# A four-layer graph network kernel: one halved group instead of two, loads in the order of need, new planned times, and a later way back in the recurrence

## The chip, the cores and the metric

The kernel runs on one core of one Trainium2 chip. The metric is the device time of one launch in microseconds (us), the median over runs. PE is TensorE, DVE is VectorE, ACT is ScalarE, POOL is GpSimd. "L306" is line 306 of the kernel whose profile is read; because the change moves lines, the same code has other numbers further down the file (the third layer's wide product is L618 in the kernel before and L627 in the changed one).

## The reference

128 graphs of 64 nodes with 256 features pass through four layers, each with a layernorm and relu ahead and a residual addition behind:

```python
for layer in (gat4, gat1, relational, gated):        # (shortened)
    h = relu(layernorm(x))
    x = x + layer(h, adj)

# gat4: softmax over neighbours, 4 heads of 64; gat1: one head of 256
# relational: only relation 1 occurs in a 0/1 adjacency:
#   relu(adj.T @ ((h W.T + b) * sigmoid(h W.T Wg.T + bg)))
# gated: three steps of
#   aggr = adj.T @ (h @ weight[i]);  h = GRU(aggr, h)
```

The three GRU steps are most of TensorE's work. They form a chain: each step needs the state of the step before.

## The kernel before

The 64 tiles of 128 rows (two graphs each) are worked on in 16 groups of 4 tiles. For each group there is a job per layer (`first_layer`, `second_layer`, `third_layer`), a job `before` (layernorm, transposes and first aggregation for the GRU), and a job `recur` (the three GRU steps). A job is a generator that emits instructions and yields its estimated TensorE time. `Weave` runs the jobs against a virtual clock: each job has a planned start and end, and the job that is most behind emits next. While the recurrence of group g is emitted, the layer jobs of group g+3 or so fill the places in between. The result is one fixed order for each engine, in which the engine then works.

```python
plan = Weave()
plan.add("weights", 14.0, 86.0, 24.0, 0.0, later_weights(early))
...
start = 103.0
for g in range(NG):
    if g < 2:                                   # groups 0 and 1 are halved
        t = 32.0 * g
        units = [(0, 2, [t + x for x in (0, 32, 60, 84)], 0),
                 (2, 2, [t + x for x in (5, 37, 65, 89)], 3 - g)]   # second half: spare tiles
    elif g < AHEAD:                             # AHEAD = 3
        units = [(0, G, [66.0, 110.0, 150.0, 185.0], 0)]
    else:
        at = 110.0 + 96.0 * (g - AHEAD)         # planned start of a group's layers
        units = [(0, G, [at + 73.0 * i for i in range(4)], 0)]
    ...
for g in range(NG):
    at = start + g * 93.0                       # planned start of a recurrence
    ...
    if g == 0:
        after += ["weights"] + spares           # its tiles lie where the spare ones lay
```

So the layers of group 3 are planned 7 us after the first recurrence's start (110 - 103), with a period of 96 us, against 93 us for the recurrences. I call this offset the phase of the plan. It drifts by 3 us a group, as far as the dependences let it.

One step of the recurrence, for chunk 0 of the new state (features 0 to 127) and then chunk 1:

```python
yield r.add(whh, hT, 0)                 # gates, 128x512 products of 0.86 us each
yield h.add(whh, hT, 0)
yield z.add(whh, hT, 0)
yield r.add(w, aT, 0)
...
yield h.add(whh, hT, 0) + h.add(whh, hT, 1)
hnat = work.tile([P, G, D], F32, name="hnat")
yield back(hnew, hnat, 0, src if last else None)    # way back: transposes (L306), copy (L308)
n = Gate("nn", 5, 2)
yield n.add(w, aT, 0) + n.add(w, aT, 1)
...
if not last:
    new = work.tile([P, K, T], F32, name="aT")
    yield along(psum, hnat, abd, new, 0)            # next aggregation (L264), copy (L268)
yield z.add(w, aT, 0) + z.add(w, aT, 1)
next(second)                                        # last half of the update of chunk 1
```

The attention vectors were loaded one after another into one tile `ab` and multiplied on GpSimd:

```python
def attention_columns(w, heads, pieces, engine):
    for i, a in enumerate(pieces):
        ab = once.tile([P, D], F32, name="ab")
        nc.scalar.dma_start(ab, over_partitions(a, D))
        wa = once.tile([P, K, D], F32, name="wa")
        engine.tensor_tensor(wa, w[:, :, :D], ab[:, None, :].to_broadcast([P, K, D]), ALU.mult)
        ...
```

## Time and profile before

| | before |
|---|---|
| median of 3 runs | 1722.49 us (1721.14 to 1729.14) |
| span of the profiled run, mean granted clock | 1725.0 us, 0.976 |
| TensorE busy | 1596.9 us (93%) |
| TensorE idle before the first recurrence matmul (161.6 us) | 53.1 us |
| TensorE idle from there to its end | 66.7 us |

Idle time of TensorE is the bracketed time ahead of each row of its timeline, summed; the bracket also names what ended it. The view of TensorE's waits collects these brackets over the run. Its columns: engine, tile and line that waited, what it waited for, us in total, times, the longest.

```profile
PE tp L166 <- DVE hn L158: 35.7, 8, 23.2
PE tp L306 <- DVE hT L330: 28.1, 15, 4.8
PE mm L250 <- DVE eb L569: 13.9, 8, 5.6
...
PE rz L295 <- DVE aT L268: 2.9, 3, 2.5
```

The first line is mostly the start: one wait of 23.2 us for the first layernorm. The second is the way back of the recurrence, waiting for the new state from DVE; with 4.9 us in which L306 waited for other things, these are the 33.0 us of the prediction. The third is the attention's aggregation, waiting for exps masked by DVE.

### The profile page before, as it was taken

To read this page: it belongs to the slowest core of one execution; us is meant where nothing else is said; L and a number is where in the kernel's file an instruction comes from. 1 tells how busy PE (TensorE), PEld (TensorE's weight loads), DVE (VectorE), ACT (ScalarE), POOL (GpSimd) and SP (SyncE) were. 2 spreads that over 40 slices of the span, in tenths; PEclk is the share of its full clock that TensorE was granted. 3 is DMA by queue.
4 is the path that set the end of the run, shared out by engine and by line. 5 is a ranking of instruction groups with operands and counts; after the bars stand their busy time and mean duration, and the time that the engine had idled before them with its cause. 6 is when DMAs were issued, how large, how long until landed. Compare 5 with 4: busy or idle time off the path is not lost.

```text
span 1725.0 us, 16160 instructions
## 1 busy us (share of the span) xinstructions
PE 1596.9 (93%) x5689; PEld 902.1 (52%) x5689; DVE 1028.4 (60%) x2401; ACT 472.8 (27%) x910; POOL 279.9 (16%) x254
## 2 busy tenths in 40 slices
PE   4877999999998998989999999999999999999997
PEld 3554555555554554545545555554555545554543
DVE  5766673856667474664647657464665657554433
ACT  2322322222322222223222332322222222222221
POOL 2110110211111011211112212021111111111110
PEclk9977999999999999999999999999999999999998
DMA  7000000000100000000000001000000000000000
GB/s 201 7 3 1 16 4 28 19 28 16 28 19 4 28 19 25 19 28 4 19 25 20 28 3 43 4 16 25 16 13 3 25 0 16 13 4 13 0 13 15
DMA packets 45510, 34.96 MB, mean 20 GB/s; under 512 B 21612, under 2 KB 43756, under 8 KB 45420
## 3 DMA queue, kind: packets, MB, share of 16 engines
q1 hardware_dynamic: 42444, 32.52, 6.7%
q10 hardware_dynamic: 2976, 1.32, 0.3%
q8 instruction: 47, 0.77, 0.2%
q14 instruction: 43, 0.35, 0.1%
HBM read 25.30 MB, written 8.52 MB: 20 GB/s over the span
## 4 chain that ended last, share of the span: by engine, by line
PE 66%; DVE 21%; POOL 5%; issue 3%; ACT 2%; DMA 2%; SPq 0%; POOLq 0%; DVEq 0%; ACTq 0%
PE rz L295 27%; PE nn L295 13%; PE mm L231 6%; PE mm L618 5%; PE mm L250 5%; PE tp L264 4%; DVE hn L158 3%; PE tp L166 3%; DVE st L149 2%; POOL rstd L154 2%; PE tp L306 2%; POOL xg L210 2%; DVE d L329 2%; DVE hT L330 1%; PE mm L630 1%
## 5 line engine op out<-in xcount | busy, mean ns | idle before, releaser
L295 PE MATMUL rz<-hT,whh 128*128 128x512 f32 x768 | 390.8, 600 | 3.9 <-ACT z L328 3.4
L295 PE MATMUL rz<-aT,wc 128*128 128x512 f32 x768 | 388.8, 597 | 3.1 <-DVE aT L268 2.9
L325 POOL TENSOR_TENSOR d<-hT,nt 128x512 f32<-128x512 f32 x96 | 125.1, 1303 | 784.1 <-ACT nt L323 784.1
L295 PEld LDWEIGHTS rz<-aT,wc 128*128 128x128 f32 x768 | 140.2, 191 | 145.4 <-issue 128.3
L295 PEld LDWEIGHTS rz<-hT,whh 128*128 128x128 f32 x768 | 138.5, 192 | 118.9 <-issue 105.5
L295 PE MATMUL nn<-aT,wc 128*128 128x512 f32 x384 | 191.1, 597 | 0.0
L295 PE MATMUL nn<-hT,whh 128*128 128x512 f32 x384 | 190.8, 598 | 0.0
L329 DVE SCALAR_TENSOR_TENSOR d<-z,d 128x512 f32<-128x512 f32 x96 | 74.2, 773 | 102.5 <-POOL d L325 59.1
L158 DVE TENSOR_SCALAR hn<-xg,mv,rstd 128x256 f32<-128x256 f32 x256 | 101.3, 441 | 46.6 <-POOL rstd L154 46.4
L264 PEld LDWEIGHTS tp<-abd,hnat 128*128 128x128 f32 x768 | 102.0, 194 | 43.3 <-issue 31.5
L618 PE MATMUL mm<-wl,hT 128*128 128x512 f32 x248 | 122.1, 617 | 0.3 <-ACT hT L167 0.3
L166 PE MATMUL tp<-ident,hn 128*128 128x128 f32 x512 | 75.5, 285 | 50.3 <-DVE hn L158 35.7
L167 ACT ACTIVATE hT<-tp 128x512 f32<-128x512 f32 (+1 forms) x130 | 69.4, 572 | 190.0 <-PE tp L166 189.8
L149 DVE BATCH_NORM_STATS2 st<-xg 128x6 f32<-128x256 f32 x256 | 98.3, 408 | 30.5 <-POOL xg L210 25.8
L250 PEld LDWEIGHTS mm<-wh,eb 128*128 128x128 f32 x600 | 87.5, 203 | 53.7 <-issue 27.8
L250 PE MATMUL mm<-wh,eb 128*128 128x65 f32 (+1 forms) x600 | 101.8, 305 | 14.5 <-DVE eb L569 13.9
L323 ACT ACTIVATE nt<-t,bi 128x512 f32<-128x512 f32 x96 | 69.2, 720 | 166.7 <-DVE t L321 141.6
L154 POOL TENSOR_TENSOR rstd<-var,mhalf 128x4 f32<-128x4 f32 (+1 forms) x70 | 68.3, 976 | 284.2 <-DVE var L153 277.8
L320 DVE SCALAR_TENSOR_TENSOR t<-r,t 128x512 f32<-128x512 f32 x96 | 67.7, 705 | 73.5 <-ACT r L317 58.7
L264 PE MATMUL tp<-abd,hnat 128*128 128x128 f32 x768 | 103.9, 278 | 3.9 <-DVE hnat L308 2.4
L317 ACT ACTIVATE r<-rz,brz 128x512 f32<-128x512 f32 x96 | 65.8, 686 | 150.4 <-PE rz L295 150.3
L166 PEld LDWEIGHTS tp<-ident,hn 128*128 128x128 f32 x512 | 61.8, 146 | 83.7 <-issue 33.1
(161 smaller groups left out, 1842.6 us busy)
## 6 DMA issues: line engine op xcount, KB each, us to landing
out_dram<-hnat SPq DMA_DIRECT2D x16, 512.0 KB
xg<-in_x_dram SPq DMA_DIRECT2D x15, 512.0 KB
hT<-row SPq DMA_DIRECT2D x26, 256.0 KB
at<-in_adj_dram SPq DMA_DIRECT2D x64, 32.0 KB
ag<-in_adj_dram SPq DMA_DIRECT2D x16, 128.0 KB
t<-row SPq DMA_DIRECT2D x26, 64.0 KB
ihn<-in_L_gnn_w_ih_dram SPq DMA_DIRECT2D x1, 768.0 KB
hhn<-in_L_gnn_w_hh_dram SPq DMA_DIRECT2D x1, 768.0 KB
```

What stands on the lines that cost most here:

```text
L149: nc.vector.bn_stats(st[:, p, :], src[:, p, :])
L154: nc.gpsimd.tensor_tensor(rstd, var, mhalf[:, :n], ALU.pow)
L158: nc.vector.tensor_scalar(hn[:, p, :], src[:, p, :], mv[:, p, 0:1], rstd[:, p : p + 1], op0=ALU.subtract, op1=ALU.mult,)
L166: nc.tensor.transpose(pt[:, p * P : (p + 1) * P], hn[:, p, k * P : (k + 1) * P], ident)
L167: nc.scalar.activation(hT[:, k, :], pt[:, : n * P], AF.Relu)
L231: nc.tensor.matmul(pm[:, : D + 2 * heads], hT[:, k, p * P : (p + 1) * P], we[:, k, :], start=(k == 0), stop=(k == K - 1),)
L250: nc.tensor.matmul(pv[:, h, :], lhsT(p, h), wv[:, p, h, :], start=True, stop=True)
L264: nc.tensor.matmul(pa[:, p * P : (p + 1) * P], hnat[:, p, c * P : (c + 1) * P], abd[:, p, :], start=True, stop=True,)
L295: nc.tensor.matmul(self.pg, w[:, k, self.chunk * P : (self.chunk + 1) * P], m[:, k, :], start=(self.done == 0), stop=(self.done == self.n ...
L325: nc.gpsimd.tensor_tensor(d, hT[:, c, :], nt, ALU.subtract)
L329: nc.vector.scalar_tensor_tensor(d, z, 1.0, d, op0=ALU.add, op1=ALU.mult)
L618: nc.tensor.matmul(pm, hT[:, k, p * P : (p + 1) * P], wl[:, k, :], start=(k == 0), stop=(k == K - 1))
```

## The change

Its intent, in its own words: only the first group is halved, so the recurrence's tiles come free in time; loads come in the order of need; the recurrence's way back of chunk 0 is later. Behind these words are five edits. (a) Group 1 is no longer halved. (b) The plan has new numbers. (c) Group 2 gets its rows by DMA (AHEAD 2). (d) The loads are reordered, with the four attention vectors in slices of one tile and their products on DVE. (e) In the recurrence `back` of chunk 0 moves behind two products, and `along` of chunk 0 moves into the next step.

```diff
+            if i > 0:
+                aT = work.tile([P, K, T], F32, name="aT")
+                yield along(psum, hnat, abd, aT, 0)
             yield r.add(w, aT, 0)
 ...
+            n = Gate("nn", 5, 2)
+            yield n.add(w, aT, 0) + n.add(w, aT, 1)
             hnat = work.tile([P, G, D], F32, name="hnat")
             yield back(hnew, hnat, 0, src if last else None)
-            n = Gate("nn", 5, 2)
-            yield n.add(w, aT, 0) + n.add(w, aT, 1)
 ...
-            if not last:
-                new = work.tile([P, K, T], F32, name="aT")
-                yield along(psum, hnat, abd, new, 0)
             yield z.add(w, aT, 0) + z.add(w, aT, 1)
 ...
-        AHEAD = 3
+        AHEAD = 2
 ...
+        AB = once.tile([P, 4, D], F32, name="AB")
+        for i, a in enumerate((a_src, a_dst)):
+            nc.scalar.dma_start(AB[:, i, :], over_partitions(a, D))
 ...
         load_group(0)
         load_group(1)
+        nc.sync.dma_start(w1e[:, :, :D], rows(W1))
 ...
-        load_group(2)
 ...
-        plan.add("weights", 14.0, 86.0, 24.0, 0.0, later_weights(early))
+        plan.add("clear", 2.5, 3.0, 0.1, 0.0, clear())
+        plan.add("columns", 2.0, 17.0, 0.2, 15.0, first_weights())
+        plan.add("weights", 18.0, 80.0, 24.0, 0.0, later_weights(early))
 ...
-        start = 103.0
+        start, period = 93.0, 93.0
 ...
+            if g == 0:
+                units = [(0, 2, (0.0, 30.0, 56.0, 76.0), False), (2, 2, (4.0, 34.0, 60.0, 80.0), True)]
+            elif g == 1:
+                units = [(0, G, (30.0, 76.0, 116.0, 146.0), False)]
+            elif g == 2:
+                units = [(0, G, (76.0, 130.0, 190.0, 235.0), False)]
             else:
-                at = 110.0 + 96.0 * (g - AHEAD)
-                units = [(0, G, [at + 73.0 * i for i in range(4)], 0)]
+                at = 130.0 + 93.5 * (g - 3)
+                units = [(0, G, [at + 68.0 * i for i in range(4)], False)]
```

More of the change, by code (lines that the diff above doesn't have):

```diff
@@ L377, in recurrence @@
             hT = hnew
-            if not last:
-                aT = new
         yield back(hT, hnat, 1, src)
@@ L448 @@
         load_group(1)
+        nc.sync.dma_start(w1e[:, :, :D], rows(W1))
+        for i, a in enumerate((a1[:D], a1[D:])):
+            nc.sync.dma_start(AB[:, 2 + i, :], over_partitions(a, D))
         wn, gn = loaded(early, "wn", W_loop), loaded(early, "gn", Wg_loop)
         ihn, hhn = loaded(early, "ihn", w_ih), loaded(early, "hhn", w_hh)
-        load_group(2)
-        wrn = [loaded(early, name, weight[i]) for i, name in enumerate(("wrn0", "wrn1", "gn"))]
+        for i, b in enumerate((b_loop, bg_loop)):
+            nc.sync.dma_start(bl[:, i * D : (i + 1) * D], over_partitions(b[0:1], D))
+        with nc.allow_non_contiguous_dma(reason="biases onto partitions"):
+            nc.sync.dma_start(bi, b_ih.rearrange("(c p) -> p c", p=P))
+            nc.sync.dma_start(bh, b_hh.rearrange("(c p) -> p c", p=P))
+        wrn = [loaded(early, name, weight[i]) for i, name in enumerate(("wrn0", "wn", "gn"))]
         make_identity(nc, ident)
@@ L459, with attention_columns @@
         nc.vector.memset(mhalf, -0.5)
-        def attention_columns(w, heads, pieces, engine):
-            for i, a in enumerate(pieces):
-                ab = once.tile([P, D], F32, name="ab")
-                nc.scalar.dma_start(ab, over_partitions(a, D))
+        def attention_columns(w, heads, pieces):
+            for i, ab in enumerate(pieces):
                 wa = once.tile([P, K, D], F32, name="wa")
-                engine.tensor_tensor(wa, w[:, :, :D], ab[:, None, :].to_broadcast([P, K, D]), ALU.mult)
+                nc.vector.tensor_tensor(wa, w[:, :, :D], ab[:, None, :].to_broadcast([P, K, D]), ALU.mult)
                 nc.vector.tensor_reduce(
@@ L471, in attention_columns @@
                 )
-        attention_columns(w0e, H, (a_src, a_dst), nc.gpsimd)
-        nc.scalar.dma_start(w1e[:, :, :D], rows(W1))
-        for i, b in enumerate((b_loop, bg_loop)):
-            nc.scalar.dma_start(bl[:, i * D : (i + 1) * D], over_partitions(b[0:1], D))
-        with nc.allow_non_contiguous_dma(reason="biases onto partitions"):
-            nc.scalar.dma_start(bi, b_ih.rearrange("(c p) -> p c", p=P))
-            nc.scalar.dma_start(bh, b_hh.rearrange("(c p) -> p c", p=P))
+        unset = []
         def blocks(name, n, pool=once):
             t = pool.tile([P, n, P], F32, name=name)
-            nc.gpsimd.memset(t, 0.0)
+            unset.append(t)
             return t
         EB = [blocks("eb0", G * H), blocks("eb1", G)]
-        OH = [blocks(f"oh{i}", G) for i in range(2)]
-        ABD = [blocks(f"abd{i}", G) for i in range(2)]
         wl = once.tile([P, K, 2 * D], F32, name="wl")
@@ L578, in attention, with clear, first_weights @@
             yield -6.0
+        def clear():
+            for t in unset:
+                nc.gpsimd.memset(t, 0.0)
+            yield 0.1
+        def first_weights():
+            attention_columns(w0e, H, (AB[:, 0, :], AB[:, 1, :]))
+            yield 0.1
+            yield -15.0
+            attention_columns(w1e, 1, (AB[:, 2, :], AB[:, 3, :]))
+            yield 0.1
         def later_weights(prep):
-            attention_columns(w1e, 1, (a1[:D], a1[D:]), nc.vector)
-            yield 0.1
             yield from relational_weights(prep, psum, wl, wn, gn, 0.5)
@@ L638 @@
         EBE = [blocks("eb0e", 2 * H, early), blocks("eb1e", 2, early)]
+        OH = [blocks(f"oh{i}", G) for i in range(2)]
+        ABD = [blocks(f"abd{i}", G) for i in range(2)]
         def first_layer(g, p0, n, spare):
@@ L670 @@
         plan = Weave()
-        plan.add("weights", 14.0, 86.0, 24.0, 0.0, later_weights(early))
+        plan.add("clear", 2.5, 3.0, 0.1, 0.0, clear())
+        plan.add("columns", 2.0, 17.0, 0.2, 15.0, first_weights())
+        plan.add("weights", 18.0, 80.0, 24.0, 0.0, later_weights(early))
         layers = (first_layer, second_layer, third_layer)
         work_of, wait_of = (9.0, 8.2, 10.4), (38.0, 35.0, 13.5)
-        users, spares = {}, []
-        start = 103.0
+        start, period = 93.0, 93.0
+        users = {}
         for g in range(NG):
-            if g < 2:
-                t = 32.0 * g
-                units = [(0, 2, [t + x for x in (0, 32, 60, 84)], 0), (2, 2, [t + x for x in (5, 37, 65, 89)], 3 - g)]
-            elif g < AHEAD:
-                units = [(0, G, [66.0, 110.0, 150.0, 185.0], 0)]
-            else:
-                at = 110.0 + 96.0 * (g - AHEAD)
-                units = [(0, G, [at + 73.0 * i for i in range(4)], 0)]
+            if g == 0:
[4 more added lines that the diff above has]
+                units = [(0, G, (76.0, 130.0, 190.0, 235.0), False)]
+            else:
+                at = 130.0 + 93.5 * (g - 3)
+                units = [(0, G, [at + 68.0 * i for i in range(4)], False)]
             for p0, n, at, spare in units:
@@ L688 @@
                     after = [(g, p0, i - 1)] if i > 0 else []
-                    if (i, i < spare) in users:
-                        after.append(users[i, i < spare])
-                    users[i, i < spare] = (g, p0, i)
-                    if i < spare:
-                        spares.append((g, p0, i))
-                    plan.add((g, p0, i), at[i], at[i + 1], work_of[i] * n / G, wait_of[i] * (1.0 if n == G else 0.0),
-                             layers[i](g, p0, n, i < spare), *after)
-        for g in range(NG):
-            at = start + g * 93.0
-            after = [(g, p0, 2) for p0 in ((0, 2) if g < 2 else (0,))] + ([("recur", g - 2)] if g > 1 else [])
-            if g == 0:
-                after += ["weights"] + spares
-            lead = 14.0 if g == 0 else 30.0
+                    if not spare:
+                        if i in users:
+                            after.append(users[i])
+                        users[i] = (g, p0, i)
+                    plan.add((g, p0, i), at[i], at[i + 1], work_of[i] * n / G, wait_of[i] * (1.0 if n == G else 0.0),
+                             layers[i](g, p0, n, spare), *after)
+            at = start + g * period
+            after = [(g, p0, 2) for p0, *_ in units] + ([("recur", g - 2)] if g > 1 else ["weights"] if g == 0 else [])
+            lead = 13.0 if g == 0 else 30.0
             plan.add(("before", g), at - lead, at, 3.3, 10.0, before(g), *after)
-            plan.add(("recur", g), at, at + 93.0, 68.0, 0.0, later(recur, g), *([("recur", g - 1)] if g else []), ("before", g))
+            plan.add(("recur", g), at, at + period, 68.0, 0.0, later(recur, g), *([("recur", g - 1)] if g else []), ("before", g))
         plan.run()
```

## The prediction

> **What bounds the kernel now.** I read the page first, then the stretches (busy time of each engine in 10 us pieces), then TensorE's waits and timeline in those pieces that are not full.
>
> ```profile
> PE 1596.9 (93%) x5689; PEld 902.1 (52%) x5689; DVE 1028.4 (60%) x2401; ACT 472.8 (27%) x910; POOL 279.9 (16%) x254
> PE   4877999999998998989999999999999999999997
> PEclk9977999999999999999999999999999999999998
> ```
>
> TensorE is the bound: it is idle for 1725.0 - 1596.9 = 128.1 us only, and the third to the fifth digit of both rows (the first 170 us) show where much of it lies, together with a low clock. Nothing that leaves TensorE's work as it is can gain more than these 128 us and what the low clock costs. Summing the idle time ahead of each TensorE row of the timeline gives 53.1 us until 161.6 us (the first matmul of the first recurrence), 66.6 us from there to 1716.5 us, and 8.4 us for the last store.
>
> ```profile
> 0.00:10.00 10.00, 0.00 (x0) 0.00 (x0) 4.83 (x18) 0.00 (x0) 6.03 (x13) 1.00 0.65 173
> 10.00:20.00 10.00, 0.00 (x0) 0.00 (x0) 2.71 (x12) 0.00 (x0) 1.08 (x2) 1.00 0.77 215
> ...
> 120.00:130.00 10.00, 7.09 (x32) 6.90 (x32) 5.55 (x14) 0.00 (x0) 0.13 (x1) 0.50 0.00 0
> ...
> 140.00:150.00 10.00, 5.94 (x11) 2.80 (x12) 8.62 (x33) 1.29 (x3) 1.70 (x2) 0.50 0.00 1
> ```
>
> Columns: stretch, length, busy us of PE, PEld, DVE, ACT, POOL, clock, DMA share, GB/s. The first 20 us hold no matmul at all, and at 120 to 150 us TensorE is partly idle and also at half clock. Two rows of the timeline say why:
>
> ```profile
> 20.49 1.26 POOL L467 TENSOR_TENSOR wa<-w0e,ab 128x512 f32<-128x512 f32 x1 [9.40 <-DMA ab<-in_L_gnn_a_dst_dram]
> ...
> 23.18 2.08 PE L166 MATMUL tp<-ident,hn 128*128 128x128 f32 x8 [23.18 <-DVE hn L158]
> ```
>
> TensorE's first work waits for a layernorm, whose power (POOL, L154) stands in POOL's order behind a multiplication that waits 9.4 us for a reloaded row ab. And:
>
> ```profile
> 101.25 0.69 DVE L631 SCALAR_TENSOR_TENSOR xg<-mm,xg 128x512 f32<-128x512 f32 x1
> ...
> 161.64 1.02 PE L295 MATMUL rz<-hT,whh 128*128 128x512 f32 x2
> ```
>
> Group 0 has passed its three layers at 101.9 us, yet its recurrence starts at 161.6 us: its tiles lie where the spare tiles of the halved groups 0 and 1 lay (the early pool is closed first), and the last matmul that reads one of those (wh1e, group 1, second half) runs at 139.9 us. In the 66.6 us after that, the waits are of this kind:
>
> ```profile
> 512.19 0.63 PE L306 MATMUL tp<-ident,hT 128*128 128x128 f32 x4 [2.50 <-DVE hT L330]
> 664.62 1.06 PE L306 MATMUL tp<-ident,hT 128*128 128x128 f32 x4 [4.82 <-DVE hT L330]
> ```
>
> L306 is the way back (transposes of the new state). 18 such waits sum to 33.0 us. By what follows them, 7 (11.4 us) are the way back of chunk 0 (512.19 is one), 11 (21.5 us) of chunk 1, above all at the end of a group (664.62).
>
> **What the Trainium skill says.** "TensorE: Matmul & The Clock Gate", Part 1: after an idle window of some 3.4 us the clock is halved until TensorE has again been busy for about that long. The trace agrees: after 5.6 us of idle before 121.8 us the clock is 0.50 and 32 matmuls of L250 take 7.09 us, where 8 take 1.00 at full clock. So a hole in the start costs about twice its first microseconds. "DMA: Bandwidth & Descriptors", Issuing engines are not separate DMA queues: transfers issued by ScalarE and SyncE share the 16 engines. The trace agrees in that the rate stays at 173 to 215 GB/s in the first 30 us with both queues in use; so moving loads between the queues changes their order, not the sum. "Perfetto Trace Analysis", Optimization Strategy: repeated bubbles on the engine that should be full can mean that the next tile finds no room. The 60 us between 101.9 and 161.6 are one bubble of this sort, not a repeated one.
>
> **The change part by part.**
>
> *Work.* Group 2 gets its rows by DMA instead of by matmuls of L540: two of 128x512 and one of 128x256 go (2 x 0.86 + 0.43 = 2.15 us, spacing from the timeline), two small transposes of L552 come (0.2 us). TensorE's work falls by 2 us. All else is moved.
>
> *Start.* Counting the built orders up to the first matmul of a recurrence, each with its spacing from the trace (transpose 0.109, 128x65 0.215, 128x128 product 0.22, 256 to 264 columns 0.43 to 0.45, 512 columns 0.86 us), gives before: 12.2 us transposes (L166, L180), 17.2 weight products (L198, L600), 20.2 values (L231), 6.7 edges and broadcasts, 13.8 aggregation (L250), 12.0 loop relation, 1.8 along: 83.9 us. These took 161.6 us, so 77.7 us were lost (53.1 idle, the rest low clock). After: 10.9 + 17.2 + 16.7 + 4.7 + 8.6 + 8.6 + 1.8 = 68.5 us. If the recurrence starts at S, the lost time is S - 68.5, and the gain is 77.7 - (S - 68.5) + 2, that is 148 - S.
>
> Now S. The four rows AB are separate slices of one tile and two of them go ahead of w0e, so the multiplication waits for no reuse, and it moves to DVE (0.69 us as for w1e, where POOL took 1.26). The first xg pieces landed at 4.4 and 6.5 us; stats, power and hn put the first transposes near 10 us instead of 23.2. But then the loads rule: in DVE's order the preparation of bh now stands before the second es of group 0, and bh comes after 4.7 MB, which at the traced rates (1.7 MB in the first 10 us, 2.15 in the next) is 24 us. So group 0's second dg matmul, at 37.5 us before, comes near 27. Its chain from there to the finished third layer took 101.9 - 37.5 = 64 us before, with DVE at 78% between 40 and 110 us. The new order puts all of group 1's first layer (16 instead of 8 aggregations, 1024-wide DVE work of 1.22 us each) ahead of group 0's second half in layer two: PE order has L250 x16 before L231 of hT1e. I follow it: transposes near 45, values to 50, dg on POOL (2.0 us) to 52.5, exps to 55, DVE 6 us to 61, aggregation to 64.5, hT1e to about 68, against 71.2 before. So most of the 10 us won are given back there. From hT1e to the end of layer three took 31 us, so group 0 is ready near 98; the way in (stats 2, power 1.3, hn 1.5, transposes 1, relu and natural copy 1.5, along 1.8 us) makes S about 107. The gain of the start is 148 - 107 = 41 us. DVE's order up to aT agrees: some 65 us of work after 26 us, at 80% gives 107.
>
> *The way back of chunk 0 later.* It moves behind two n matmuls of 0.86 us. Of the seven waits (2.36, 1.67, 1.05, 2.50, 2.28, 1.34, 0.22) 1.72 us each go: 2.0 us stay, 9 are won. Moving along (L264) of chunk 0 to the next layer puts it before the r product that reads aT: along's end to aT took 0.95 us at 1676.35. In the new order something of 0.5 to 1.7 us mostly stands between (nn, the back of chunk 1, or a wl product), so I take 3 us of new waits. Net 6 us.
>
> Sum: 41 + 6 = 47 us, less 1 for hazards of a new interleaving: 1722.5 - 46 = 1676.5, say 1677 us.
>
> **Rivals.** (1) *DVE and the static order keep the start long.* For it: DVE is above 70% between 40 and 100 us; group 1's whole width stands in group 0's way. S would be 125, the time 1722.5 - 23 - 6 = 1694. Against it: there is less work in all before the recurrence. (2) *The loads take the place of the removed wait*: ag of group 0 now comes after 6.3 MB (31 us), and DVE's oh that needs it stands before the second eb. It would cost 3 to 8 us: 1680 to 1685. (3) *The late along exposes aT's copy* in all 32 layer changes with up to 0.95 us, more where DVE is in a 1.2 us instruction: 30 us lost, 1701. Against it: the scheduler has put other matmuls between. (4) *The group-end waits grow or go*: the 4.82 us wait at 664.6 comes from the next layernorm's hn standing before L329 in DVE; with all jobs shifted, the 66.6 us of idle could become 40 or 85. (5) *All goes well*: S of 95 and few waits, 1655.
>
> **Range and chances.** The start's S between 97 and 122 gives 15 us up or down, the later waits some 15 more, mostly independent: about 20 us together for 8 in 10. Range 1655 to 1702. The 2% line is 1688.0, about 0.7 of a standard deviation above 1677. Chances: faster 0.75, same 0.24, slower 0.01.
>
> **What would show it.** First transposes near 10 us and second dg matmul near 27 (the start of the loads); first L295 at 97 to 122, with no long hole between xg of layer three and it (the tiles); TensorE busy about 1590 us, as there are fewer half-clock stretches; the waits L306 on hT falling from 33 to some 24 us in sum, and rz on aT (2.9 us in three) below 6. I am wrong if the first recurrence starts after 130 us, or if idle time from there to the end is above 90 us.

## The result, and the profile after

| | before | after |
|---|---|---|
| median of 4 runs each | 1723.0 us (1721.14 to 1729.14) | 1666.53 us (1666.04 to 1670.05) |
| profiled span, clock | 1725.0, 0.976 | 1665.0, 0.987 |
| first recurrence matmul, S | 161.6 us | 125.5 us |
| TensorE work emitted ahead of it | 83.9 us | 68.5 us |
| lost in the start (S less that work) | 77.7 us | 57.0 us |
| TensorE idle before S / after S | 53.1 / 66.7 us | 36.7 / 37.2 us |
| busy time lost to the low clock before S / after S | 14.7 / 12.8 us | 10.4 / 4.3 us |
| L306 waits, all kinds | 33.0 us | 2.9 us |

The ratio is 0.9671 (95% interval 0.9643 to 0.9698): faster. The clock row is, for stretches of 10 us, the busy time times one less the granted clock, summed up to the last products of the recurrence.

The median fell by 56.5 us where 46 were predicted, and 1666.5 is inside the range. The table shows that this is not the predicted sum. The start gave 77.7 - 57.0 = 20.7 us of lost time (and the 2 us of saved work), not 41. From S to the end, idle time fell by 29.5 us and the low clock took 8.5 us less: 38 us, where 5 had been predicted. Two errors of opposite sign met.

The changed kernel's page:

```profile
PE 1582.6 (95%) x5683; PEld 896.8 (54%) x5683; DVE 1008.5 (61%) x2384; ACT 470.2 (28%) x896; POOL 273.1 (16%) x245
...
PE   6779999999999999999999999999999999999997
...
PEclk9799999999999999999999999999999999999999
```

The 8s in the middle of TensorE's row of before are gone (its slices 13, 16 and 18, of 43 us each, so between about 520 and 780 us). Busy time fell by 14.3 us; 12.8 of these are the low clock of the table, so only about 1.5 us are less work.

The stretches (length, busy us of PE, PEld, DVE, ACT, POOL, clock, DMA share, GB/s) show the start:

```profile
0.00:10.00 10.00, 0.00 (x0) 0.00 (x0) 3.00 (x15) 1.28 (x1) 3.92 (x10) 1.00 0.70 174
10.00:20.00 10.00, 4.65 (x13) 3.02 (x14) 8.78 (x27) 1.58 (x5) 3.64 (x12) 1.00 0.80 243
...
60.00:70.00 10.00, 3.25 (x12) 1.61 (x10) 7.30 (x12) 3.03 (x11) 2.40 (x2) 0.88 0.06 13
70.00:80.00 10.00, 9.13 (x36) 7.95 (x37) 5.11 (x15) 1.44 (x2) 0.13 (x1) 0.50 0.01 2
```

TensorE now begins inside the second stretch. But a new hole stands at 60 to 70 us, where TensorE works 3.25 us of 10, and the next ten microseconds run at half clock. TensorE's timeline (start, us, then what, with the idle time before it) names it:

```profile
14.80 1.23 PE L166 MATMUL tp<-ident,hn 128*128 128x128 f32 x4 [14.80 <-DVE hn L158]
...
70.39 7.09 PE L250 MATMUL mm<-wh,eb 128*128 128x65 f32 x32 [5.41 <-DVE eb L568]
...
82.69 2.01 PE L231 MATMUL mm<-w1e,hT1e 128*128 128x258 f32 x8
...
125.48 1.02 PE L295 MATMUL rz<-hT,whh 128*128 128x512 f32 x2
```

The 32 matmuls of L250 are group 1's whole first layer (16 products in the code, two records each; group 0's 32 had run by 43.6 us). They wait 5.41 us for exps that DVE masks in 1024-wide pieces; group 0's own next products (hT1e) stand behind them, at 82.69. The waits of TensorE after the change, in the columns of before:

```profile
PE tp L166 <- DVE hn L158: 26.0, 7, 14.8
...
PE mm L250 <- DVE eb L568: 12.3, 9, 5.4
PE rz L295 <- DVE aT L268: 7.0, 10, 1.3
PE tp L306 <- DVE hT L330: 2.3, 1, 2.3
```

The second line of before, L306 on hT, went from 28.1 us in 15 waits to 2.3 in one. Why it did is the main question of the experiments.

### The profile page after: what moved, and what is told of

The parts are those of the page before. It is cut to its first block, busy times and chain, and to the rows that moved or that the text cites. A ratio compares the mean times of both kernels' runs of the same rounds, so it can differ in the third digit from the quotient of the medians.

```text
span 1665.0 us, 16128 instructions
## 1 busy us (share of the span) xinstructions
PE 1582.6 (95%) x5683; PEld 896.8 (54%) x5683; DVE 1008.5 (61%) x2384; ACT 470.2 (28%) x896; POOL 273.1 (16%) x245
## 4 chain that ended last, share of the span: by engine, by line
PE 77%; DVE 14%; POOL 3%; issue 2%; ACT 2%; DMA 1%; SPq 0%; ACTq 0%; DVEq 0%; POOLq 0%
PE rz L295 34%; PE nn L295 15%; PE mm L627 6%; PE mm L231 6%; PE mm L250 5%; PE tp L264 3%; PE tp L166 3%; PE tp L306 2%; DVE hn L158 2%; PE mm L639 2%; DVE st L149 2%; DVE eb L568 1%; POOL xg L210 1%; DVE hn L209 1%; POOL rstd L154 1%
## 5 line engine op out<-in xcount | busy, mean ns | idle before, releaser
L329 DVE SCALAR_TENSOR_TENSOR d<-z,d 128x512 f32<-128x512 f32 x96 | 66.0, 688 | 119.2 <-ACT z L328 65.6
L149 DVE BATCH_NORM_STATS2 st<-xg 128x6 f32<-128x256 f32 x256 | 98.8, 403 | 48.0 <-POOL xg L210 41.9
L158 DVE TENSOR_SCALAR hn<-xg,mv,rstd 128x256 f32<-128x256 f32 x256 | 101.5, 441 | 39.6 <-POOL rstd L154 39.3
L264 PEld LDWEIGHTS tp<-abd,hnat 128*128 128x128 f32 x768 | 101.3, 195 | 39.7 <-issue 29.4
L250 PEld LDWEIGHTS mm<-wh,eb 128*128 128x128 f32 x620 | 89.1, 199 | 57.4 <-issue 31.2
L627 PE MATMUL mm<-wl,hT 128*128 128x512 f32 x248 | 118.3, 600 | 0.4 <-ACT hT L167 0.4
L250 PE MATMUL mm<-wh,eb 128*128 128x65 f32 (+1 forms) x620 | 103.5, 300 | 12.9 <-DVE eb L568 12.3
L295 PEld LDWEIGHTS nn<-aT,wc 128*128 128x128 f32 x384 | 71.3, 190 | 78.6 <-issue 75.1
L328 ACT ACTIVATE z<-rz,brz 128x512 f32<-128x512 f32 x96 | 65.8, 685 | 147.5 <-PE rz L295 147.5
L319 ACT ACTIVATE t<-nn,bh 128x512 f32<-128x512 f32 x96 | 65.8, 686 | 146.9 <-PE nn L295 146.9
L264 PE MATMUL tp<-abd,hnat 128*128 128x128 f32 x768 | 103.1, 280 | 2.7 <-DVE fT L553 2.6
```

What stands on the lines that cost most here:

```text
L149: nc.vector.bn_stats(st[:, p, :], src[:, p, :])
L158: nc.vector.tensor_scalar(hn[:, p, :], src[:, p, :], mv[:, p, 0:1], rstd[:, p : p + 1], op0=ALU.subtract, op1=ALU.mult,)
L250: nc.tensor.matmul(pv[:, h, :], lhsT(p, h), wv[:, p, h, :], start=True, stop=True)
L264: nc.tensor.matmul(pa[:, p * P : (p + 1) * P], hnat[:, p, c * P : (c + 1) * P], abd[:, p, :], start=True, stop=True,)
L295: nc.tensor.matmul(self.pg, w[:, k, self.chunk * P : (self.chunk + 1) * P], m[:, k, :], start=(self.done == 0), stop=(self.done == self.n ...
L329: nc.vector.scalar_tensor_tensor(d, z, 1.0, d, op0=ALU.add, op1=ALU.mult)
```

## The experiments

Twelve kernels were run, each with one profiled and three timed runs beside runs of the kernel before on the same chip; all were correct. Runs 1 to 4 share a median of before of 1726.16 us, 5 to 8 one of 1724.25, 9 to 11 one of 1724.2, and 12 one of 1722.91.

### 1. The recurrence's moves alone, in the kernel before

```diff
 # kernel before, with edit (e) only
+            if i > 0:
+                aT = work.tile([P, K, T], F32, name="aT")
+                yield along(psum, hnat, abd, aT, 0)
             yield r.add(w, aT, 0)
 # ... and back(hnew, ...) behind the two n products
```

> The kernel before with the two moves in the recurrence alone (way back of chunk 0 behind the n products, along of chunk 0 into the next layer); start and plan as before. Theory A (the moves themselves take the waits of the way back away, of both chunks): waits of L306 on hT fall from 33 us to under 10 us, idle time of TensorE after the first recurrence matmul from 66.7 to about 42 us, time about 1697 us. Rival B (the new plan shifted the layers' work against the recurrence, and that removed the waits of chunk 1 at the ends of groups): the 21.5 us of chunk 1 stay, only some 9 us of chunk 0 go, time about 1713 us. In both the first recurrence matmul stays near 161 us.

Measured: 1737.42 us, ratio 1.0066 (1.0035 to 1.0096). Both theories fell: the kernel became 11 us slower. Its waits of TensorE:

```profile
PE tp L306 <- DVE hT L330: 24.3, 10, 5.4
PE mm L250 <- DVE eb L567: 24.1, 12, 5.6
PE rz L295 <- DVE aT L268: 10.2, 10, 2.2
```

The ways back won 5 us (33.0 to 28.1 over all kinds of wait), half of what had been worked out for chunk 0, and their longest wait is still 5.4 us. But the aggregation now waits 24.1 us for eb where it waited 13.9, and the recurrence 10.2 for aT where it waited 2.9. TensorE's idle time after S is 71.9 us instead of 66.7, and the low clock takes 20.3 us instead of 12.8.

### 2. The changed kernel without them

```diff
 # changed kernel, edit (e) undone: back and along where they were
```

> The changed kernel with the two moves in the recurrence undone; start and plan as changed. Theory A: the waits of L306 on hT come back to 25 to 33 us, idle time after the first recurrence matmul from 37.2 to about 62 us, time about 1692 us. Rival B: only the waits of chunk 0 come back (some 9 to 11 us), those at the ends of groups stay away, time about 1676 us. First recurrence matmul near 125 us in both.

Measured: 1677.89 us, ratio 0.9719 (0.9689 to 0.9749), against 1666.53 for the changed kernel: in the new plan the same moves are worth 11.4 us by the medians (8 by the ratios, whose intervals overlap a little; the ranges of the runs do not). L306 waits 10.3 us in all here, far from 33, so most of these waits had gone before the recurrence was touched. The sign of edit (e) is therefore set by the kernel around it: 11 us lost in the old one, 8 to 11 won in the new one. That it is the planned times in this kernel, and not the loads or the start, is not tested alone; run 5 speaks for it, as its waits for hT, eb and aT (29.2, 24.0 and 10.6 us) are much like those of run 1 (24.3, 24.1 and 10.2).

### 3. The tiles freed, in the kernel before

If group 1's second half uses no spare tiles, nothing of group 1 has to be done before the first recurrence.

```diff
-                 (2, 2, [t + x for x in (5, 37, 65, 89)], 3 - g)]
+                 (2, 2, [t + x for x in (5, 37, 65, 89)], 3 if g == 0 else 0)]
```

> The kernel before, but the second half of group 1 no longer takes the spare tiles (it waits for the first half's); halves, loads, plan and recurrence as before. Theory (the 60 us between the end of group 0's third layer and its recurrence are the spare tiles of group 1): the recurrence starts within 15 us of the end of group 0's third layer, at 110 to 128 us instead of 161.6, and the time falls by 12 to 22 us, to 1700 to 1710 us. Rival (the late start is the work and the loads ahead of it, the tiles only look guilty): the start stays above 145 us and the time above 1714 us.

Measured: 1729.33 us, ratio 1.0016 (0.9985 to 1.0047): the same. On DVE, group 0's last residual addition of the third layer:

```profile
96.90 0.69 DVE L631 SCALAR_TENSOR_TENSOR xg<-mm,xg 128x512 f32<-128x512 f32 x1 [0.23 <-PE mm L630]
```

And TensorE afterwards:

```profile
131.76 8.88 PE L250 MATMUL mm<-wh,eb 128*128 128x65 f32 x36 [5.99 <-DVE eb L569]
...
144.60 2.07 PE L295 MATMUL rz<-hT,whh 128*128 128x512 f32 x2 [0.52 <-ACT hT L167]
```

Group 0 is ready at 97.6 us and its recurrence starts at 144.6, with its tiles free. What stands between is TensorE's own order: the second half of group 1 and the first layer of group 2 were planned ahead, in part at half clock, and the 36 matmuls of L250 wait 6 us for eb. This is the reading of the 60 us hole in the prediction, refuted: the tiles were not what held the recurrence back. That S came 17 us earlier gave nothing: what had been emitted ahead of S fell by 12.4 us as well (83.9 to 71.5), to be done later, and the 4.6 us that the start lost less went in idle time and low clock after S (68.0 and 17.3 us, where they were 66.7 and 12.8) and in the spread of the runs.

### 4. Group 1 out of group 0's way, in the changed kernel

```diff
-                units = [(0, G, (30.0, 76.0, 116.0, 146.0), False)]
+                units = [(0, G, (50.0, 96.0, 126.0, 156.0), False)]
```

> The changed kernel with group 1's first two layers planned 20 us and its third 10 us later, so that in TensorE's order the products of group 0's second half in layer two (hT1e) stand ahead of group 1's first aggregation (L250 x16). Theory (group 1's whole width in the way costs group 0 about 15 us): hT1e's products end near 70 us instead of 84.7, the first recurrence matmul comes at 108 to 115 us instead of 125.5, the time falls by 8 to 14 us, to 1653 to 1659 us. Rival (the lost time only moves: group 1 is late for recurrence 1, or the same holes come elsewhere): the start comes earlier but the time stays within 4 us of 1666.5.

Measured: 1654.83 us (1649.22 to 1655.68), ratio 0.9576 (0.9542 to 0.9610). It beats both kernels: 11.7 us below the changed one by the medians, some 16 by the ratios, whose intervals do not meet. Its TensorE timeline, to be set beside the rows at 82.69 and 125.48 above:

```profile
60.76 2.01 PE L231 MATMUL mm<-w1e,hT1e 128*128 128x258 f32 x8
...
110.32 1.09 PE L295 MATMUL rz<-hT,whh 128*128 128x512 f32 x2
```

Group 0's products come 22 us earlier, S 15 us earlier, and the lost time of the start is 45.7 us instead of 57.0. These 11.3 us account for the 11.6 between the two profiled spans (1665.0 and 1653.4); idle time after S hardly moved (37.8 against 37.2).

### 5. The old phase, in the changed kernel

```diff
-                at = 130.0 + 93.5 * (g - 3)
-                units = [(0, G, [at + 68.0 * i for i in range(4)], False)]
+                at = 100.0 + 96.0 * (g - 3)
+                units = [(0, G, [at + 73.0 * i for i in range(4)], False)]
```

100 is 7 us after the planned start of 93, as 110 was after 103.

> The changed kernel, but groups 3 to 15 planned as before against their recurrences: first layer at 100 + 96 us per group (was 110 + 96 with a start at 103, now the start is 93), layers 73 us apart, instead of 130 + 93.5 and 68. Start and recurrence as changed. Theory C (the plan's phase keeps layernorms of the next group out of the way of the recurrence's last updates and is worth some 18 us): idle time after the first recurrence matmul rises from 37.2 to about 55 us, with waits of L306 on hT at the ends of groups back, time about 1683 us. Rival D (the phase has no part in it, undivided group 1 and the earlier start did it): 37 us of idle stay, time 1663 to 1670 us.

Measured: 1719.79 us, ratio 0.9975 (0.9956 to 0.9993). The direction was right and the size far larger than expected: this one edit to the numbers of the plan takes back 53 of the 56.5 us, though S (124.3 us) and the start's lost time (55.8) stay as in the changed kernel. All of it comes later: idle after S 77.8 us instead of 37.2, low clock 20.2 us instead of 4.3. The row of TensorE in its page, and the line of its waits:

```profile
PE   6779989999998988999999999999999999999997
```

```profile
PE tp L306 <- DVE hT L330: 29.2, 12, 5.4
```

The 8s are back, in the slices 6, 13, 15 and 16, and so are the long waits for the state. It is more than the phase costs alone, as this kernel also has edit (e), which run 1 showed to lose 11 us at this phase.

### 6. The new phase, in the kernel before

```diff
-                at = 110.0 + 96.0 * (g - AHEAD)
-                units = [(0, G, [at + 73.0 * i for i in range(4)], 0)]
+                at = 140.0 + 93.5 * (g - AHEAD)
+                units = [(0, G, [at + 68.0 * i for i in range(4)], 0)]
```

140 is 37 us after 103, as 130 is after 93.

> The kernel before, but groups 3 to 15 planned as in the changed one against their recurrences: first layer at 140 + 93.5 us per group (10 us later than in the changed one, as the start is 103 and not 93), layers 68 us apart. Theory C: idle time after the first recurrence matmul falls from 66.7 to about 48 us, above all the L306 waits at the ends of groups (21.5 us), time about 1704 us. Rival D: idle stays at 62 to 70 us, time 1720 to 1728 us. First recurrence matmul near 161 us in both.

Measured: 1699.71 us, ratio 0.9871 (0.9847 to 0.9895): 24.5 us won by three numbers, within 2% and yet the largest single part found. S is still 159.3 us and the start loses 75.9. Idle after S fell from 66.7 to 49.1, the low clock after S from 12.8 to 4.6 us. Its page and its waits:

```profile
PE   4877999999999999999999999999999999999997
```

```profile
PE tp L306 <- DVE hT L330: 9.2, 12, 2.3
```

The start is that of before, all behind it is that of after. L306 waits 11.6 us in all, and no wait is longer than 2.3 us.

### 7 and 8. The loads alone, and the changed kernel without them

```diff
 # 7: kernel before with edit (d): AB tile, order of loads, first_weights, clear
 # 8: changed kernel with the old loads and the old attention_columns
```

> The kernel before with the changed loads alone: the attention rows in one tile and first, their multiplication on DVE, w1e and the biases in the order of need on SyncE, POOL's memsets as a job of the plan; groups 0 and 1 halved, group 2 by matmuls, plan and recurrence as before. Theory E (the earlier first transposes, 14.8 instead of 23.2 us, carry through to the first recurrence): first recurrence matmul at 152 to 156 us, time 1715 us. Rival F (the start is bound by the chain through the halved groups and by what stands in the order, the 8 us are filled up again): first recurrence matmul within 3 us of 161.6, time 1720 to 1727 us.

> The changed kernel with the loads as before (attention row tile reloaded, POOL's multiplication ahead of the first layernorm's power, w1e and biases on ScalarE's queue); group 1 undivided, plan and recurrence as changed. Theory E: first transposes near 23 us, first recurrence matmul near 133 us instead of 125.5, time 1674 us. Rival F: the loss is filled up by later holes, first recurrence matmul within 3 us of 125.5, time 1664 to 1669 us.

Measured: 1713.85 us for 7, ratio 0.9941 (0.9925 to 0.9958), so 10.4 us won in the kernel before; 1674.80 us for 8, ratio 0.9715 (0.9699 to 0.9731), so 8.3 us lost when they are taken out of the changed kernel. In the start, 7 loses 69.6 us instead of 77.7, and 8 loses 65.5 instead of 57.0. The loads are worth some 8 to 10 us in either setting, and add to the rest.

### 9. Only the later way back, with along at its old place

```diff
 # changed kernel, half of edit (e) undone
+            if not last:
+                new = work.tile([P, K, T], F32, name="aT")
+                yield along(psum, hnat, abd, new, 0)
             yield z.add(w, aT, 0) + z.add(w, aT, 1)
```

> The changed kernel with only one of the recurrence's two moves: the way back of chunk 0 stays behind the n products, but the product along of chunk 0 goes back into the z stage of the layer before. Theory G (the late way back alone takes the waits of L306 away, the late along only costs waits on aT): L306 waits stay near 3 us, waits of rz on aT fall from 7.0 to about 3 us, time 1660 to 1665 us. Rival H (along in the z stage now stands too close behind the later way back, so that the two moves need each other): waits of L264 on hnat come up by 8 us or more, time 1673 to 1680 us, near the 1677.9 us without both.

Measured: 1673.57 us, ratio 0.9702 (0.9685 to 0.9718). L306 waits 3.1 us against 10.3 in run 2, so moving `back` does what it is for; its 4.3 us in time are less certain, as the intervals of the two ratios overlap. Moving `along` as well gives another 7 us by the medians, 5 by the ratios, whose intervals overlap too. The prediction had booked that move as a cost of 3 us. The mechanism expected for the gain, `along` no longer waiting for hnat, is not seen: L264 waits for hnat in 1.3 us only. Most of the difference is in idle time after S, 43.7 against 37.2 us, in small pieces at many places; what it is made of stays open.

### 10. A phase 8 us earlier, on top of run 4

```diff
-                at = 130.0 + 93.5 * (g - 3)
+                at = 122.0 + 93.5 * (g - 3)
```

> The kernel with group 1 later (1654.8 us), and groups 3 to 15 planned 8 us earlier: first layer at 122 + 93.5 us per group. In the built order no way back is now followed within 1.6 us of TensorE's work by more than one psum tile of other transposes (15 places at 130). Theory C (what counts is where the layers' work falls against the recurrence's updates, and the 14 us of waits of L166 on hnat come from that): these waits fall below 4 us, idle time after the first recurrence matmul from 37.8 to 20 to 25 us, time 1638 to 1644 us. Rival (other waits take their place, as the order on DVE decides and not that on TensorE): idle stays above 33 us, time 1651 to 1660 us.

Measured: 1688.62 us (1680.06 to 1690.83), ratio 0.9775 (0.9745 to 0.9805), 34 us slower than run 4 and outside both ranges expected. This is the one run that shifts the offset of the layers alone, with period and spacing kept. The theory behind it had looked at TensorE's order: the largest wait left was that of the next layernorm's transposes for the recurrence's hnat (14.3 us), as both use the tp buffers by that theory, and in the built order of 122 the two no longer follow each other. That came true, this wait is 0. But a larger one took its place:

```profile
PE tp L306 <- DVE hT L330: 37.9, 24, 3.2
```

The order that matters is DVE's. Its timeline at the end of a group in run 10:

```profile
432.44 0.65 DVE L329 SCALAR_TENSOR_TENSOR d<-z,d 128x512 f32<-128x512 f32 x1
434.01 0.41 DVE L158 TENSOR_SCALAR hn<-xg,mv,rstd 128x256 f32<-128x256 f32 x1 [0.91 <-POOL rstd L154]
434.34 0.68 DVE L330 SCALAR_TENSOR_TENSOR hT<-d,nt 128x512 f32<-128x512 f32 x1
```

and TensorE behind it:

```profile
435.08 0.66 PE L306 MATMUL tp<-ident,hT 128*128 128x128 f32 x4 [2.54 <-DVE hT L330]
```

L329 and L330 are the last two steps of the new state. Between them stands an L158 of another group's layernorm, which waits for its power from POOL; DVE idles 0.91 us, the state comes late, and TensorE waits 2.54 us. In the kernel before the same place looks as follows:

```profile
661.61 0.73 DVE L158 TENSOR_SCALAR hn<-xg,mv,rstd 128x256 f32<-128x256 f32 x2 [1.19 <-POOL rstd L154]
662.26 0.69 DVE L329 SCALAR_TENSOR_TENSOR d<-z,d 128x512 f32<-128x512 f32 x1
...
663.79 0.68 DVE L330 SCALAR_TENSOR_TENSOR hT<-d,nt 128x512 f32<-128x512 f32 x1
```

and in the changed kernel:

```profile
428.94 0.18 DVE L252 RECIPROCAL rec<-mm 128x4 f32<-128x4 f32 x1 [1.97 <-PE mm L250]
429.04 0.67 DVE L329 SCALAR_TENSOR_TENSOR d<-z,d 128x512 f32<-128x512 f32 x1
...
429.96 0.68 DVE L330 SCALAR_TENSOR_TENSOR hT<-d,nt 128x512 f32<-128x512 f32 x1
```

In the changed kernel the neighbours of the state are an aggregation's reciprocal and product (L252, L253), in all groups but the last three, which have no such layer beside them, and DVE is free for the state in time: the L306 at 431.37 us has no idle time before it. In the kernel before the neighbour changes from group to group, as the phase drifts, and here it is a layernorm in wait for POOL.

The traces allow a count over all 16 groups: the time from the end of the last z (ACT, L328) of a group to the end of its L330.

| kernel | this time, all 16 groups |
|---|---|
| changed | 1.5 to 2.1 us |
| before with the new planned times (run 6) | 1.5 to 1.9 us |
| before | 1.5 to 7.3 us, above 3 us in groups 4 to 8 |
| changed with the old planned times (run 5) | 1.5 to 6.7 us, above 3 us in groups 0, 4, 5, 7 and 8 |
| run 10 | 3.1 to 4.8 us in groups 0 to 12, 1.5 us in the last three |

So the state is late where other work stands ahead of or between L329 and L330 on DVE. A layernorm in wait for POOL is one case of it, not the rule: in run 10 it stands between the two in groups 1 to 3 only, with 8.0 of the 44.0 us that L306 waits in all; in groups 4 to 9 it is statistics (L149, L150), which wait for nothing there. In the kernel before it stands ahead or between in groups 4 and 5, and in groups 7 and 8 a step of the elu (L209) stands ahead.

### 11. Group 1 later still

```diff
-                units = [(0, G, (30.0, 76.0, 116.0, 146.0), False)]
+                units = [(0, G, (60.0, 106.0, 131.0, 161.0), False)]
```

> The changed kernel with group 1's first two layers planned 30 us and its third 15 us later. Before the first recurrence matmul stand only 58.4 us of TensorE's work (64.6 at 20 us later, 68.5 as changed). Theory (what is lost is the time before that matmul less the work in it; the chain of group 0 now meets little else): first recurrence matmul near 98 us, lost time 40 us against 45.7 at 20 us later, time near 1649 us. Rival (with less work beside the chain TensorE idles and its clock falls, and group 1 comes late for recurrence 1): lost time 46 us or more, time 1655 to 1662 us.

Measured: 1660.23 us, ratio 0.9633 (0.9615 to 0.9650), better than the changed kernel (6 us by the medians and also by the ratios, whose intervals just overlap), not better than run 4. S is 100.9 us and the start loses 42.5 us, 3.2 less than run 4, but idle after S is 40.8 us instead of 37.8. Of the three settings tried (as changed, 20 and 30 us later) 20 is the fastest.

### 12. Group 1 halved again, in the changed kernel

```diff
-                units = [(0, G, (30.0, 76.0, 116.0, 146.0), False)]
+                units = [(0, 2, (32.0, 64.0, 92.0, 116.0), False), (2, 2, (37.0, 69.0, 97.0, 121.0), True)]
 # second half on spare tiles for layers 0 and 1, and the first recurrence waits for these
```

> The changed kernel, but group 1 in halves again, its second half on the spare tiles in the first two layers, planned 32 us behind group 0 as before; the first recurrence therefore has to wait for these tiles. Loads, later groups' plan and recurrence as changed. Before the first recurrence matmul stand 79.2 us of TensorE's work instead of 68.5. Theory K (the undivided group 1 with its tiles free is worth some 10 us of the start): first recurrence matmul at 146 to 152 us, so 67 to 73 us lost ahead of it instead of 57.0, time 1676 to 1682 us. Rival L (the halves only move work ahead of the recurrence; freeing the tiles is worth nothing by itself, as the run with free tiles in the kernel before): first recurrence matmul near 136 us, 55 to 60 us lost, time 1663 to 1670 us.

Measured: 1669.14 us, ratio 0.9688 (0.9663 to 0.9712); the interval overlaps that of the changed kernel (0.9643 to 0.9698). S is 139.0 us, but 79.2 us of work stand ahead of it, so the start loses 59.8 us against 57.0. The part that gives the change its name is worth about 3 us here, a difference within the intervals.

## Why the prediction was right or wrong

**The time** was right, and two of its terms were wrong in opposite directions. Of the 60.0 us between the profiled spans the start gave 22.7 with the saved work instead of 41, and what follows 38 instead of 5. The right time is in part luck. The working itself has two small slips: 68 and 31 us make 99, where it says 98, and "53.1 idle, the rest low clock" does not hold for the 77.7 us lost, since the low clock took 14.7 of the other 24.6. The 9.9 us that are neither stand in the changed kernel as well (57.0 less 36.7 and 10.4), so they do not touch the gain.

**Start: first transposes near 10, second dg near 27.** The wait for the reloaded row is gone, but the first transposes came at 14.8 us: in DVE's order other preparations (masks, squared weights, diagonals, the products with w0e) stand before hn, whose power was ready at 9.2 us. The second dg matmul, at 37.5 us before, came at 30.3, 3 us late:

```profile
30.31 1.02 PE L539 MATMUL mm<-dg0e,same 128*128 128x512 f32 x2
```

**Start: "hT1e to about 68".** This is the step that failed. The rows at 70.39 and 82.69 show it: hT1e came at 82.7 to 84.7. The prediction had seen that group 1's whole width stands in the way and had priced the path to the end of it too low, by 16.7 us. Its own steps show where. Group 1's values ended at 59.7 us instead of 50; of these 9.7 us, 3.3 are the late second dg matmul, and the rest lies ahead of and in the transposes and values, which ran at a granted clock of 0.66 (50 to 60 us). Dg, exps and DVE's pieces took 10.6 us, where 11 were assumed. The aggregations, at half clock, were over at 77.5 us, 7.1 us later, where 3.5 were assumed. From there to the end of hT1e it took 7.2 us, where 3.5 were assumed, with L180, L609 and L250 of other jobs between. The steps behind it held. From the end of hT1e to the finished third layer it took 32.4 us where 31 were assumed, as DVE shows,

```profile
116.44 0.69 DVE L640 SCALAR_TENSOR_TENSOR xg<-mm,xg 128x512 f32<-128x512 f32 x1 [0.30 <-PE mm L639]
```

and the way in took from 117.1 to 125.5, 8.4 us where 9 were assumed. So 107 + 16.7 + 1.4 - 0.6 makes 124.5 of the measured 125.5 us; the last microsecond is the slip in the sum. Run 4 confirms it from the other side: with group 1 out of the way hT1e is at 60.8 us, S at 110.3, and the profiled span falls by what the start loses less, 11 us. The first rival (S of 125) had the right S, and would have had the right start; its time of 1694 fell with the other error.

**Start: the tiles.** "its tiles lie where the spare tiles of the halved groups 0 and 1 lay" is true and explains nothing of the time: with the tiles free (run 3) nothing was won, with them bound again (run 12) about 3 us were lost. "One bubble" was a misreading, too: in the 59.7 us from 101.9 to 161.6 TensorE was busy for 41.2 us, at a mean granted clock of 0.71. The hole was for the most part work that TensorE's fixed order put ahead of the recurrence. That the gain of a start is its lost time, and not S, was a sound step of the prediction: run 3 moved S by 17 us and the time by nothing.

**Loads.** The second rival (loads take the place of the wait) fell: the loads are worth 8 to 10 us in both settings (runs 7 and 8).

**Way back: "Net 6 us".** As an account of edit (e) it fails in both plans: -11 us in the old one (run 1), +8 to +11 in the new one (run 2). The term for aT was sized well, 7.0 us where 2.9 + 3 were expected; that for the way back came to 4.9 us in run 1 and to 7.4 in the new plan (10.3 to 2.9), where 9 were expected. The step that failed is the silent one, that all other waits would stay: in run 1 the waits of L250 for eb rose from 13.9 to 24.1 us. That the moved products shifted what stands beside them on DVE is a reading and was not tested. The third rival, 30 us lost to the late `along`, fell.

**Later waits.** The 21.5 us at the ends of groups were left in the sum as they were; "(4) The group-end waits grow or go" named what would happen, with 40 or 85 us of idle time. They went: 37.2 us. The cause is shown by runs 5 and 6 to be the plan of groups 3 to 15. Its three numbers, offset, period and spacing, are worth 24.5 us in the kernel before, and taking them back costs 53 us in the changed kernel. These runs move the three together, so they do not tell the phase from the other two; run 10 moves the offset alone and loses 34 us, which shows that the phase by itself can be worth as much. The count in run 10 shows how it acts at the ends of the groups: the last two steps of the state come late on DVE in before, in run 5 and in run 10, and in time in after and in run 6. No run moved these instructions alone on DVE, and what share of the idle time the ends of the groups account for was not worked out.

**The sum** of the tested parts: planned times 24.5 (run 6), recurrence 8 to 11 (run 2), loads 8 (run 8), halving about 3 (run 12): 44 to 47 of 56.5 us. The other 9 to 13 are in edits not run alone, as group 2's rows by DMA, the window of the weights and the earlier start of 93, and in the parts' effect on each other, which runs 1 and 5 show to be large. This stays open.

**Falsifiers.** S was not after 130 us and idle time not above 90, and TensorE's busy time (1582.6) is near 1590. Five signs did not fit: the first transposes (14.8 us, not 10), the second dg matmul (30.3, not 27), S outside 97 to 122, L306 (2.9 us, not 24) and the waits for aT (7.0 us, not below 6). S and L306 could be read at once, and would have shown an offsetting pair even without experiments.

## What to carry to other kernels

Where a fixed plan weaves two streams, their relative phase is a parameter of its own: sweep it before judging any local edit, since it can decide the edit's sign. Judge an order by the engine that makes what the bound engine waits for (here DVE), and look for other jobs' operations, in wait or not, just ahead of and between the last steps of the critical chain. And weigh a faster start by its lost time, not by the moment at which the next stage begins.

## What the Trainium skill lacked or had wrong

- "Perfetto Trace Analysis", Optimization Strategy, suggests interleaving stages and looking at gaps on the bound engine. It does not say that the relative phase of two interleaved streams can be worth more than the edits to either: 24.5 us for the planned times in run 6, and 34 us for a shift of the offset by 8 us in run 10.
- The same section offers missing buffers as the meaning of repeated bubbles, and the prediction applied this to one large bubble. Runs 3 and 12 show a bubble where free tiles change the time by nothing and by about 3 us. "TensorE: Matmul & The Clock Gate", Part 2, step-by-step, has the better reading, that matmuls stay in program order: in run 3 the ready recurrence (97.6 us) waits until 144.6 us behind matmuls of other groups.
- "TensorE: Matmul & The Clock Gate", Part 1, gives about 3.4 us of idle time for the clock to fall and about as much work for it to return. In run 4 a hole of 2.73 us ahead of the 32 matmuls of L250 was enough for half clock (0.79 granted from 70 to 75 us, 0.50 from 75 to 80), and in the kernels before, after and of run 4 it stayed at 0.50 for the whole 7.09 us of these 32 matmuls of 128x65. The page speaks of a budget of time, whatever is issued; 7 us of such narrow matmuls did not bring the clock back.
